# Two transformer blocks on one core: soft-MoE jobs interleaved with their neighbours, six PSUM banks in one ring

## The chip, the core and the metric

The kernel runs on one core of a Trainium2 chip. A core has five engines that run beside each other, each with an instruction queue of its own that it works off in order: TensorE (PE in the profile; its weight loads are listed as PEld), VectorE (DVE), ScalarE (ACT), GpSimd (POOL) and SyncE (SP, which here only issues DMAs). Matmul results go to PSUM, which holds eight banks of 128 partitions x 512 float32; every result has to be read out of its bank by DVE or ACT before the bank can take another.

The metric is the device time of one execution in microseconds; lower is better. The kernel before took 1081.13 us, the median of three runs (1080.82 to 1083.46).

## The reference

The input `x` is 8 sequences of 512 tokens, 128 channels. Two blocks follow each other; each normalises its input and adds the outputs of an attention and of a feed-forward part that both read the normalised rows. All is float32.

```python
xn = layernorm(x)
x = x + causal_attention_16_heads(xn) + soft_moe(xn)
xn = layernorm(x)
x = x + differential_attention(xn) + attention_and_top2_moe(xn)
```

The change touches the soft MoE of the first block. It has 8 experts of 64 slots each, so 512 slots:

```python
xn2 = rmsnorm(xn, norm_gamma);  sn = rmsnorm(slot_embeds, slot_norm_gamma)
logits   = einsum('bnd,esd->bnes', xn2, sn)      # per sequence: 512 tokens x 512 slots
dispatch = softmax(logits, over the tokens n)
combine  = softmax(logits, over all slots (e, s))
slots = einsum('bnd,bnes->besd', xn2, dispatch)
h  = gelu(einsum('besd,edh->besh', slots, w1) + b1)
eo = einsum('besh,ehd->besd', h, w2) + b2
out = einsum('bmd,bnm->bnd', eo, combine)
```

## The kernel before, in words

The program is written out in full by Python, in the order in which the code runs, and `in_order` (L244) ties every engine's instructions of the first part to that order. So the order in the text is the order on PE, DVE, ACT and POOL; what can differ is only how long each waits.

**Jobs.** For each of the 8 sequences (called batches, `b`) the soft MoE is two jobs. `dispatch(b)` (L326) returns five steps: `start` transposes the normalised rows (four 128x128 transposes into one bank, `xn2T_p`) and copies them to SBUF on ACT; `logits(k)` calls `soft` (L310) for blocks k and k+1: a matmul of 128 slots x 512 tokens into a bank (`lg`), the negated maximum of each row on DVE (`nm`), the exponential with its row sum on ACT (`ex`); `scale(k)` divides two blocks by their sums on DVE; `turn(k)` transposes two blocks (four transposes each into a bank, `dt`) and copies them on ACT into `disp`; `end` multiplies the rows by `disp` (`psl`, four matmuls that accumulate in a bank of the pool `o`) and writes the slots `slT` on DVE. `combine(b)` (L370) is alike with tokens as rows: `logits`, no scaling, `turn` (`ct`, copied to `comb` by ACT and DVE in turn) and `end`, which multiplies by the experts' outputs (`pf`) and adds to `x_all` on DVE.

Each `logits` or `turn` step handles two of the four blocks, so a job has two of each, with k = 0 and k = 2.

**The order of jobs.** `jobs` (L405) is a generator that runs a list of jobs as a pipeline of depth two: while `new` computes its logits, `last` is turned and ended. Each `yield` is a point at which others put in work of their own. `begin` (L415) starts the next dispatch, `rows_of` (L411) normalises the rows of the one after.

**Where jobs run.** Five stages, by their callers:
1. L542: dispatch 0 to 3, woven with `rest_in`, the layernorm statistics of batches 3 to 7. `weave` (L230) takes one step of each generator in turn.
2. L544: `slot_ffn(0)` (L454), the experts for the slots of batches 0 to 3, woven with dispatch 4 and 5 and with `late_in` (L517).
3. L545 to L590: the weights of the second block are folded, then combine 0, dispatch 6, combine 1, dispatch 7.
4. L592: `slot_ffn(1)` woven with combine 2 and 3.
5. L1163 to L1198: combine 4 to 7, with tiles from the pool `t`, beside the preparation of the first block's attention. The string at L1165 gives the order: each `p` is one piece of the preparation of batch 0 (`PREP`, L1019), each `c` one step of `jobs`; from L1194 four steps of `jobs` follow each group of four `m_head` calls (L1042, `sm`), until the jobs are done. There are nine such groups (`AHEAD`) before the first `e_head` (L1073, `se`), with which the attention proper begins. The preparation reduces squares and takes three Newton steps on DVE, transposes `q` and `k` (`qT_p`, `kT_p`), and ACT makes `qT` and `kj` of them.

**PSUM.** Three pools serve stages 1 to 4: `s` with four banks for logits and for the experts' hidden layer (`ph`), `o` with two banks for sums that build up over several matmuls (`psl`, `pf`, `pe`), `t` with two banks for transposes. A pool is a ring: a new tile takes the oldest bank and its first writer waits until that bank's last tile has been read. Stage 5 and the attention have other pools: seven banks `t` and one `o`.

The order of the steps in one round of `jobs` is this: both turns of `last`, then both logits of `new`, then the end of `last`:

```python
for k in (0, 2):
    if last: last[3](k); yield          # turn
for k in (0, 2):
    if new: new[1](k); ...; yield       # logits
if last: last[4](); yield               # end
```

Of the kernel before, what the change touches and what calls it, by code (L numbers as in the profile page):

```python
# [25 lines left out]
def kernel(ctx: ExitStack, tc: tile.TileContext, a: dict, out: bass.AP):  # L26
# [21 lines left out]
    ps = {}  # L48
# [189 lines left out]
                    runs.remove(r)  # L238

    fp = ExitStack()  # L240
    for k, n in (("s", 4), ("o", 2), ("t", 2)):
        ps[k] = fp.enter_context(tc.tile_pool(name=f"ps_{k}", bufs=n, space=PSUM))

    def in_order(start, end=None):  # L244

        free = mybir.DependencyInfo(mybir.DependencyClass.NoSync, mybir.DependencyReason.DATA)
        last = {}
        for ins in list(nc.cur_bb.bb.instructions)[start:end]:
            if ins.engine in engines:
                if ins.engine in last:  # L250
                    tc.add_manual_dep(ins, last[ins.engine], free, reason="order of the trace")
                last[ins.engine] = ins.name
# [69 lines left out]
    def xn2_in(b):  # L322
        ff["xn2", b] = xn2 = wkb.tile([P, NI, D], F32, tag="xn2", name=f"xn2_{b}", bufs=3)
        ln_apply0(b, 1, xn2)
# [80 lines left out]
    def jobs(todo):  # L405

        last = None
        ds = [b for kind, b in todo if kind is dispatch]
        made = {}

        def rows_of(b):  # L411
            if b is not None and ("xn2", b) not in ff:
                xn2_in(b)

        def begin(b):  # L415
            if b is not None and b not in made:
                rows_of(b)
                made[b] = dispatch(b)
                made[b][0]()

        def after_(b):
            n = ds.index(b) + 1 if b in ds else len(ds)
            return ds[n] if n < len(ds) else None

        if todo[0][0] is dispatch:
            begin(ds[0])
        for kind, b in todo + [(None, None)]:
            new = made[b] if kind is dispatch else kind(b) if kind else None
            nxt = None
            if kind is dispatch:  # L430
                nxt = after_(b)
            elif kind and ds and b is not None:
                nxt = next((d for d in ds if d not in made), None)
            for k in (0, 2):
                if last:
                    last[3](k)
                    yield
            for k in (0, 2):
                if new:
                    new[1](k)  # L440
                    if k == 0:
                        begin(nxt)
                    else:
                        rows_of(after_(nxt))
                        new[2](0)
                    yield
            if new:
                new[2](2)
            if last:
                last[4]()  # L450
                yield
            last = new
# [87 lines left out]
    ln_rows(2)  # L540
    ln_roots(2)
    weave((0, jobs([(dispatch, b) for b in range(HB)])), (1, rest_in()))  # L542
    l1_load()
    weave((0, slot_ffn(0)), (0, jobs([(dispatch, 4), (dispatch, 5)])), (0, late_in(range(6))))  # L544
    l1_fold()  # L545
    ac = {}
# [43 lines left out]
    for _ in jobs([(combine, 0), (dispatch, 6), (combine, 1), (dispatch, 7)]):  # L590
        pass
# [331 lines left out]
    with ExitStack() as at:  # L923
# [14 lines left out]
        for n in range(3):  # L938
            t = pads.tile([P, NI, PW * (2 * H + 1)], F32, name=f"vpad{n}")
# [3 lines left out]
        for n in range(4):  # L943
            t = pads.tile([P, NI, P], F32, name=f"mcol{n}")
# [636 lines left out]
```

## Time and profile before

| | |
|---|---|
| median of three runs | 1081.13 us (1080.82 to 1083.46) |
| profiled execution, its own time | 1080.87 us |
| its span, first to last instruction | 1079.2 us, mean granted clock 0.945 |
| stage 1, 10.4 to 64.1 us | 53.7 us, PE busy 43.27 |
| stage 2, 64.1 to 115.9 | 51.8 us, PE busy 49.66 |
| stage 3, 115.9 to 162.5 | 46.6 us, PE busy 39.74 |
| stage 4, 162.5 to 212.7 | 50.2 us, PE busy 48.20 |
| stage 5, 212.7 to 280.6, up to the first `se` | 67.9 us, PE busy 63.47 |
| a logit matmul (two passes of 592 ns that overlap), its maximum, its exponential | 0.86, 0.69, 0.69 us |
| four transposes into a bank, their copy on ACT | 0.52, 0.59 us |
| a table load on ACT (before a switch between exponential and Gelu) | 1.28 us |

How to read the profile: the page gives busy time by engine and in 40 slices of 27 us, with the granted clock of PE in tenths of full speed. A timeline lists an engine's instructions in order of time: start in us, duration in us, engine, line, operation, output and inputs with their shapes, how many were merged, and in brackets how long the engine stood idle before and which instruction ended that. Names leave out numbers (`dt` is any `dt_0_1`), and L141 is the line of the helper that records all transposes. A table of stretches gives the busy time of each engine in each stretch and the clock. Matmuls overlap in the pipeline, so durations of single ones do not add up; what adds up is the distance from start to start.

### The profile page before, as it was taken

Reading aid. Unit: us, or ns where it says so; the run is one execution under the profiler, and the core shown is the slowest. Engines: PE = TensorE matmul, PEld = TensorE weight load, DVE = VectorE, ACT = ScalarE, POOL = GpSimd, SP = SyncE. Lnnn points to the kernel's source line nnn. Section 1 sums busy time; section 2 is a strip of 40 time slices with the busy share of each in tenths; the row PEclk is TensorE's granted clock in tenths of the full one; section 3 lists DMA queues with packets and bytes.
Section 4 is the critical chain, followed back from the end, with each engine's and each line's share of the span. In section 5 each row is a group of like instructions: output and inputs, shape, how many; then the busy total and the mean of one; then the engine's idle time right before and its main releaser. Section 6 shows DMA issues by size and latency. Waiting matters only on the chain.

```text
span 1079.2 us, 18766 instructions
## 1 busy us (share of the span) xinstructions
PE 964.9 (89%) x6702; PEld 594.3 (55%) x6702; DVE 677.6 (63%) x2130; ACT 561.3 (52%) x1261; POOL 569.0 (53%) x794
## 2 busy tenths in 40 slices
PE   7889899989999999999899999878678879999990
PEld 3457556857545455545444445345445657777780
DVE  6634643377777788888878788359887642243230
ACT  3466347363366566767565655526346552393220
POOL 3201000200242537785878978876877635667775
PEclk9899999999699999999999999859889999999995
DMA  8630000000000000000000000050000143332213
GB/s 253 153 92 2 1 1 1 2 1 2 1 1 2 1 2 2 19 4 2 9 14 2 22 1 22 2 173 1 10 20 16 30 110 58 50 50 36 26 10 34
DMA packets 49838, 33.23 MB, mean 31 GB/s; under 512 B 12248, under 2 KB 44803, under 8 KB 49744
## 3 DMA queue, kind: packets, MB, share of 16 engines
q1 hardware_dynamic: 34832, 24.80, 8.6%
q0 software_dynamic: 14096, 6.97, 4.9%
q8 instruction: 53, 0.87, 0.3%
q14 instruction: 41, 0.34, 0.1%
q10 hardware_dynamic: 816, 0.26, 0.1%
HBM read 17.56 MB, written 17.33 MB: 32 GB/s over the span
## 4 chain that ended last, share of the span: by engine, by line
PE 62%; POOL 13%; DVE 13%; issue 5%; ACT 3%; DMA 2%; POOLq 0%; SPq 0%; DVEq 0%; ACTq 0%
PE se L1082 11%; PE phm L1458 6%; PE pem L1473 6%; PE po L1107 5%; PE sm L1049 4%; PE lg_d L316 3%; PE pe L491 3%; PE psl L360 3%; DVE junk L1059 3%; PE s L1287 3%; PE pf L393 2%; POOL xs L910 2%; PE pq L969 2%; PE lg_c L316 2%; PE ph L465 2%
## 5 line engine op out<-in xcount | busy, mean ns | idle before, releaser
L1059 DVE CUSTOM_DVE_ANT_0 junk<-sm,cmask 128x128 f32<-128x128 f32 (+3 forms) x512 | 249.7, 488 | 68.9 <-PE sm L1049 30.5
L1087 ACT ACTIVATE pt<-se 128x384 f32<-128x384 f32 (+1 forms) x384 | 185.7, 527 | 158.7 <-PE sm L1049 110.0
L1049 PE MATMUL sm<-kj,qT 32*128 32x256 f32 (+3 forms) x1024 | 231.5, 483 | 5.4 <-ACT kj L643 2.7
L1082 PE MATMUL se<-q,kj 32*128 32x128 f32 (+3 forms) x1024 | 210.2, 477 | 4.0 <-DVE mcol L1059 3.5
L1486 POOL DMA_INDIRECT out_dram<-es,to x80 | 124.4, 1555 | 61.9 <-issue 28.4
L1082 PEld LDWEIGHTS se<-q,kj 32*128 32x128 f32 x1024 | 99.8, 189 | 86.9 <-DVE mcol L1059 25.2
L1092 POOL TENSOR_SCALAR_AFFINE_SELECT pt<-pt 128x512 f32<-128x512 f32 (+1 forms) x96 | 80.0, 833 | 115.2 <-ACT pt L1087 115.0
L1049 PEld LDWEIGHTS sm<-kj,qT 32*128 32x128 f32 x1024 | 111.4, 190 | 24.4 <-DVE mcol L1059 10.3
L1107 PE MATMUL po<-pt,vpad 128*18 128x512 f32 (+3 forms) x1024 | 92.0, 455 | 12.0 <-POOL pt L1092 12.0
L1461 ACT ACTIVATE hTm<-phm 128x1024 f32<-128x1024 f32 (+1 forms) x48 | 42.4, 882 | 79.0 <-PE phm L1458 78.8
L1458 PE MATMUL phm<-xeT,w 128*128 128x512 f32 (+1 forms) x192 | 78.7, 534 | 4.1 <-DVE xeT L1447 3.6
L1473 PEld LDWEIGHTS pem<-w,hTm 128*128 128x128 f32 x640 | 77.0, 192 | 7.6 <-issue 7.2
L1291 ACT ACTIVATE ex<-s,nm 128x512 f32<-128x512 f32 x64 | 43.9, 687 | 69.2 <-DVE nm L1290 68.7
L1473 PE MATMUL pem<-w,hTm 128*128 128x128 f32 x640 | 78.9, 275 | 0.0
L910 POOL DMA_INDIRECT xs<-l_z,sput x64 | 67.3, 1051 | 17.9 <-issue 15.4
L1287 PE MATMUL s<-xn,qk 128*128 128x512 f32 x128 | 69.4, 662 | 7.1 <-ACT qk L1265 3.9
L522 POOL TENSOR_TENSOR x_all<-x_all,bo_bc 128x512 f32<-128x512 f32 x8 | 10.2, 1276 | 121.4 <-DVE xn L280 121.4
L1447 DVE TENSOR_SCALAR xeT<-xeT_p,cols 128x512 f32<-128x512 f32 (+1 forms) x24 | 17.2, 721 | 73.9 <-PE xeT_p L141 73.9
L1107 PEld LDWEIGHTS po<-pt,vpad 128*18 128x18 f32 x1024 | 20.7, 97 | 62.8 <-POOL pt L1092 23.7
L1290 DVE TENSOR_REDUCE nm<-s 128x1 f32<-128x512 f32 x64 | 43.0, 683 | 17.0 <-PE s L1287 16.7
L1458 PEld LDWEIGHTS phm<-xeT,w 128*128 128x128 f32 x192 | 34.0, 194 | 27.0 <-issue 21.6
L736 POOL TENSOR_TENSOR l_prod<-l_qkv 128x512 f32<-128x512 f32 x36 | 46.3, 1298 | 3.2 <-DVE l_at L630 1.9
(270 smaller groups left out, 1872.4 us busy)
## 6 DMA issues: line engine op xcount, KB each, us to landing
xs<-cmask SPq DMA_DIRECT2D x1, 5280.0 KB, 24.1
xe<-xs SPq DMA_DIRECT2D x8, 660.0 KB, 4.4
x_all<-in_L_attn_x_dram SPq DMA_DIRECT2D x8, 256.0 KB, 4.6
w<-in_L_ffn_w_dram SPq DMA_DIRECT2D x1, 2048.0 KB, 8.9
w<-in_L_ffn_moe_w_dram SPq DMA_DIRECT2D x1, 2048.0 KB, 9.8
out_dram<-x_all SPq DMA_DIRECT2D x8, 256.0 KB, 2.2
out_dram<-es,to POOLq DMA_INDIRECT x80, 3.2
xs<-l_z,sput POOLq DMA_INDIRECT x64, 2.3
```

Of the source, the lines that this page charges most:

```text
L316: nc.tensor.matmul(lg, lhsT=lhs(k), rhs=rhs, start=True, stop=True)
L910: put = nc.gpsimd.indirect_dma_start(out=xs, out_offset=bass.IndirectOffsetOnAxis(ap=sput[:, k, m : m + 1], axis=0), in_=z2[:, i], in_offs ...
L1049: nc.tensor.matmul(sc[:, o : o + w], lhsT=st["qT", b][rr, i * P : (i + 1) * P], rhs=st["k", b, j][rr, :w], start=True, stop=True,)
L1059: nc.vector.tensor_tensor_reduce(out=junk[:, :w], in0=sc[:, o : o + w], in1=cmask[:, 512 - w : 512], scale=-1.0, scalar=BIG, op0=ALU.add, ...
L1082: nc.tensor.matmul(sc[:, o : o + w], lhsT=st["k", b, j][rr, c * P : (c + 1) * P], rhs=st["q2", b, (g % G) // 2][rr, c * P : T], start=True ...
L1087: nc.scalar.activation(st["pt", g, k][:, r, :o], sc[:, :o], AF.Exp)
L1092: nc.gpsimd.affine_select(out=pt[:, :, :n, :P], in_=pt[:, :, :n, :P], pattern=[[0, 4], [0, n], [1, P]], compare_op=ALU.is_ge, fill=0.0, ba ...
L1107: nc.tensor.matmul(po[32 * r : 32 * r + 2 * PW, c * P : T], lhsT=vpads[b % 3][:, c, at_ : at_ + 2 * PW], rhs=pt[:, r, o : o + w], start=(c ...
L1287: nc.tensor.matmul(sc, lhsT=dd["qk", b, k][:, i * P : (i + 1) * P], rhs=xnT[:, b], start=True, stop=True)
L1458: nc.tensor.matmul(ph[:, k, :w], lhsT=w1_1[:, e, hc * P : (hc + 1) * P], rhs=xeT[:, :w], start=True, stop=True)
L1473: nc.tensor.matmul(pe[:, k * D : (k + 1) * D], lhsT=hT[:, hc, k * P : (k + 1) * P], rhs=w2_1[:, e, hc, :], start=(hc == 0), stop=(hc == NH ...
L1486: back = nc.gpsimd.indirect_dma_start(out=out_rows, out_offset=bass.IndirectOffsetOnAxis(ap=ee["to", e][:, c : c + 1], axis=0), in_=es[:, ...
```

## The change

It has two parts.

The pools `s` and `t` of stages 1 to 4 become one ring of six banks; `ps["s"]` is another name for it. So logits, the experts' hidden layer and transposes take banks in the order in which they are written in the program.

The round of `jobs` is reordered: first half of `new`'s logits, first turn of `last`, `begin` of the next dispatch, second turn of `last`, second half of `new`'s logits with the scaling and the rows of the one after, end of `last`. A round with both jobs now has six yields, where it had five, since `begin` has one of its own (also when there is nothing to begin). The weaving callers and the string at L1165 are as before, so their own steps fall between other steps of the jobs than before.

```diff
     fp = ExitStack()
-    for k, n in (("s", 4), ("o", 2), ("t", 2)):
+    for k, n in (("o", 2), ("t", 6)):
         ps[k] = fp.enter_context(tc.tile_pool(name=f"ps_{k}", bufs=n, space=PSUM))
+    ps["s"] = ps["t"]
...
-            for k in (0, 2):
-                if last:
-                    last[3](k)
-                    yield
-            for k in (0, 2):
-                if new:
-                    new[1](k)
-                    if k == 0:
-                        begin(nxt)
-                    else:
-                        rows_of(after_(nxt))
-                        new[2](0)
-                    yield
+            if new:
+                new[1](0)
+                yield
+            if last:
+                last[3](0)
+                yield
+            if new:
+                begin(nxt)
+                yield
+            if last:
+                last[3](2)
+                yield
+            if new:
+                new[1](2)
+                new[2](0)
+                rows_of(after_(nxt))
+                yield
             if new:
                 new[2](2)
             if last:
```

## The prediction

> **What bounds the kernel now.** I read the page first, for who is busy and at what clock; then the stretches table, cut at the borders of the stages that the change touches; then PE's timeline in those stages; then DVE's and ACT's, to see what PE waits for; last, the granted clock in steps of about 3.4 us around each halving.
>
> ```profile
> PE 964.9 (89%) x6702; PEld 594.3 (55%) x6702; DVE 677.6 (63%) x2130; ACT 561.3 (52%) x1261; POOL 569.0 (53%) x794
> PE   7889899989999999999899999878678879999990
> PEclk9899999999699999999999999859889999999995
> ```
>
> PE is busy for 89% of the span, and the first ten slices (27 us each) are no exception. Only its idle time and its slow clock can be won. The stages follow; columns are the stretch, its length, then busy us of PE, PEld, DVE, ACT and POOL, the granted clock, DMA.
>
> ```profile
> 10.40:64.10 53.70, 43.27 (x148) 23.52 (x148) 35.44 (x121) 24.70 (x54) 10.81 (x7) 0.90 0.81 203
> 64.10:115.90 51.80, 49.66 (x396) 36.34 (x396) 22.59 (x58) 32.69 (x65) 8.60 (x9) 1.00 0.01 2
> 115.90:162.50 46.60, 39.74 (x197) 25.39 (x196) 26.80 (x70) 23.26 (x53) 0.20 (x1) 1.00 0.00 1
> 162.50:212.70 50.20, 48.20 (x433) 39.21 (x433) 15.52 (x34) 28.18 (x58) 7.90 (x12) 1.00 0.00 1
> 212.70:280.60 67.90, 63.47 (x357) 43.70 (x357) 49.85 (x147) 27.72 (x72) 8.08 (x21) 0.90 0.00 1
> ```
>
> I call them S1 (dispatch jobs 0-3), S2 (slot experts, dispatch 4-5), S3 (fold, two combines, two dispatches), S4 (slot experts, combines 2-3) and S5 (combines 4-7 beside the preparation of the attention). PE stands idle 10.4, 2.1, 6.9, 2.0 and 4.4 us in them, and in S1 and S5 part of its work ran at half clock. From 280.6 on the order is the same in both kernels. PE's timeline shows where it waits (start, us, work, idle before it and who ended it):
>
> ```profile
> 33.67 1.07 PE L141 MATMUL dt<-ident,ex_d 128*128 128x128 f32 x8 [1.97 <-DVE ex_d L343]
> 36.24 1.94 PE L141 MATMUL dt<-ident,ex_d 128*128 128x128 f32 x8 [1.50 <-DVE ex_d L343]
> 37.97 3.62 PE L316 MATMUL lg_d<-xn2T,snT 128*128 128x512 f32 x4
> 43.83 3.60 PE L360 MATMUL psl<-disp,xn 128*128 128x512 f32 x8
> 53.01 3.60 PE L360 MATMUL psl<-disp,xn 128*128 128x512 f32 x8
> ...
> 72.38 1.00 PE L141 MATMUL xn2T_p<-ident,xn 128*128 128x128 f32 x4 [1.13 <-DVE xn L280]
> 128.07 1.10 PE L141 MATMUL ct<-ident,ex_c 128*128 128x128 f32 x8 [1.27 <-ACT comb L385]
> 172.87 1.98 PE L316 MATMUL lg_c<-snT,xn2T 128*128 128x512 f32 x4 [0.83 <-ACT hT L471]
> 232.47 1.51 PE L1049 MATMUL sm<-kj,qT 32*128 32x512 f32 x8 [2.70 <-ACT kj L643]
> ```
>
> In S1 the transposes wait for DVE's scaling (L343), which stands behind the layernorm statistics of later batches. The logits at 37.97 took 3.62 us where the pair takes 1.88 at full clock. The clock in the two places:
>
> ```profile
> 31.70:35.10 3.40, 1.07 (x9) 0.86 (x8) 3.15 (x14) 0.71 (x2) 0.00 (x0) 1.00 0.19 53
> 35.10:38.50 3.40, 2.26 (x9) 2.10 (x10) 3.19 (x15) 1.23 (x3) 1.00 (x1) 0.51 0.48 114
> 229.70:233.10 3.40, 0.70 (x9) 0.31 (x8) 1.53 (x5) 3.40 (x8) 0.00 (x0) 1.00 0.00 0
> 233.10:236.50 3.40, 3.40 (x20) 2.59 (x13) 2.10 (x6) 1.91 (x3) 0.00 (x0) 0.50 0.00 0
> ```
>
> A stretch of 3.4 us with about 1 us of PE work is followed by one at 0.50; each such stretch full of PE work costs 1.7 us.
>
> **The change, part by part.** Durations from the timelines: a logit 0.86 us of PE, its maximum 0.64 of DVE back to back, its exponential 0.69 of ACT (0.86 with the sum); four transposes 0.52, their copy 0.53; `psl` 3.44; `pf` 3.57. No instruction of these is added or removed; PE's, DVE's and ACT's are reordered. POOL's and SP's queues keep their order, and no DMA moves. ACT loads its table four times less (4 x 1.28 = 5.1 us), two in each slot stage; I cost that at nothing, as PE runs without a gap from 73.2 to 115 and ACT waits for it. Should PE wait there for `hT`, it would be worth up to 1.3 us each.
>
> The added waits: a neighbour's first two maxima now stand on DVE, and its first two exponentials on ACT, ahead of the copies of the job's own transposes. Behind those copies waits `psl` or `pf` on PE.
>
> *S1: -3.5.* I follow the new queues with the old durations. DVE: the first two maxima end at 15.9; statistics of batch 3 1.7; two maxima 1.3; scaling 1.05; the next rows 1.1; roots 0.3; scaling 1.05; job 1's two maxima 1.3: 23.5. ACT then ends their exponentials at 24.5 and makes five copies (four of `dt`, one of `xn2T`, 2.65): `psl` of job 0 starts at 27.2 (before 28.10). DVE goes on with two batches of statistics (4.0), two maxima 1.3, scaling 1.05, rows 1.1, statistics 1.7, scaling 1.0, slots 0.75 and roots 0.3, two maxima 1.3: 35.95. ACT adds exponentials and five copies: `psl` of job 1 at 39.7 (before 43.83). Job 2 is near PE's own pace: logits 1.72, four transposes 2.0, logits 1.72 and 0.25 of wait give 48.85 (before 53.01). The last one comes 2.85 us after the end of that (52.3): 55.15, before 59.59. So -4.4, if PE's clock is full throughout. As 1.07 us of transposes in a stretch was too little to keep the clock (31.7 to 35.1), I expect one or two halved stretches here too, mostly beside waits: 0 to 2 us back. Bounds -4.4 and -0.5 (a halved stretch under a whole `psl` as well); I take -3.5, nearer to the walk than to the clock's worst.
>
> *S2: -1.1.* Slots' up matmuls now stand where PE waited 1.13 us for the rows of batch 5. The 0.97 us ahead of the first logits (69.27) stays. The ring of six never stands: the bank six tiles back is read out several us earlier at each step.
>
> *S3: -1.25.* The 1.13 us at 123.20 stays, since the first combine has no neighbour. The 1.27 at 128.07 goes, and 0.24 to 0.29 at each second pair of transposes (four banks more). Late next is ACT: job 6's copies wait for the next job's exponentials, which costs 0.4 ahead of `psl`. Walked through, the four ends come 0.85, 0.7, 1.0 and 1.25 us earlier. Bounds -1.7 and -0.6.
>
> *S4: -1.2.* The waits of 0.35 (170.04) and 0.83 for a bank go: the ring is two deeper than the four that experts and logits shared.
>
> *S5: +3.0.* The combines now give three turns where they gave two, but the attention's pieces take seven turns as before. So `pf` of job 4 (3.57) and half of job 5's logits (1.72) move behind the first `sm`: 5.3 us. In front of it DVE's chain decides: last square at 219.3, sum and small steps 1.7, two maxima 1.3, Newton 3.6, two maxima 1.3, `q` 0.6, a copy 0.75, `k` 0.6: 229.1. Only two exponentials, two copies, `qT` 0.77 and `kj` 0.70 are left on ACT: `sm` starts at 230.65 (before 232.47). PE then has 5.3 - 1.8 = 3.5 us more to do up to the last `pf`. After that one group of `sm` fewer remains (2.84 of DVE) and no sum of squares (1.7), so the end of this sum is the old one within 0.7. But PE does only transposes between 220.9 and 230.65. That is two or three stretches like 229.7 to 233.1, so the clock stays halved until about 236.5: 5.9 us at half, of which 1.2 us is more than before's 3.4; and the combines' maxima and `sm`'s reductions meet each other on DVE, about 1 to 2.5 us by walking both queues. Bounds 0 and +5; I take +3.
>
> [...]
>
> From 280.6 on the work only shifts, but the halved stretch 270.6 to 287.7 covers 7.1 us of dense work there; it may end a stretch sooner or later: +-1.7, taken as 0.
>
> Sum: -3.5 - 1.1 - 1.25 - 1.2 + 3.0 = -4.05 on the profiled execution's 1080.87 (span 1079.2 and 1.67 around it): 1076.8. That execution lies 0.26 under the median 1081.13: **1077.1**.
>
> **Rivals.** 0.3%, about what a measurement of this kernel can tell from no change, is 3.2 us: 1077.9 and 1084.4 are the marks.
>
> *Flat.* S1 is bound by DVE's order and not by PE's, as its walk for job 0 shows (0.9 us won only); with S1 at its bound of -0.5 the sum is -1.05: 1080.1. For it: DVE was 3.15 of 3.4 us busy at 31.7. Against: the scaling comes up to 4 us earlier for job 1.
>
> *More.* S5 at its bound 0, S1 at -4.4: sum -7.95, 1073.2. For it: ACT had four exponentials ahead of `kj`. Against: the empty stretch on PE.
>
> *Slower: the clock.* Each job now waits in the ring for banks that its neighbour's exponentials hold (in S1's job 1 the last transposes wait 1.5 us), with only transposes around it. If that halves the clock in the dispatch and combine jobs, every stretch costs 1.7. It decides against the change from the third extra stretch on (4.05 / 1.7); five give 1077.1 + 8.5 = 1085.6. Against: in 130 to 160 us PE already stopped 0.24 to 0.29 us at each pair, at clock 1.00. [...]
>
> *Not what it says.* Five tiles of one job fill the ring, so interleaving hides nothing and each stage stays as it was; S5's shift alone would show: 1081 to 1084, part of the flat case.
>
> **Numbers.** Forecast 0.47, its own range 1074 to 1077.9; more 0.08; flat with the last 0.30; slower 0.15. So faster 0.55, same 0.30, slower 0.15. The range 1071.5 to 1084.4 leaves out the slower case and the far end of "more" (0.04).
>
> **What would show it.** S1's last `psl` at 54 to 57; no idle of 1.13 at `xn2T_p` in S2 and none of 0.83 at `lg_c` in S4; 26 table loads; in S5 idle of 4 us on PE ahead of `qT_p`, the first `sm` earlier and the clock at 0.50 after it; the first `se` 3 to 5 us earlier than 280.6. Wrong it is if S1 ends as before (DVE's order), if S5 gives away more than 5, or if halved stretches appear in S3.

## The result and the profile after

The changed kernel takes 1074.91 us (median of five runs, 1070.79 to 1079.17), the kernel before 1081.13: a ratio of 0.9934, 95% interval 0.9908 to 0.996. Measured once more in another group of runs it was 0.9922 (0.9908 to 0.9936). The runs of the kernel before lie at medians of 1081.1 to 1088.6 in the groups below, so kernels of different groups are compared by their ratios alone.

The profiled execution of the changed kernel is one of its longer runs, 1078.73 us (span 1077.0): the two profiles lie 2.14 us apart, the medians 6.22. The page's busy times, and PE's slices with the clock:

```profile
PE 967.1 (90%) x6702; PEld 595.5 (55%) x6702; DVE 676.2 (63%) x2130; ACT 553.5 (51%) x1257; POOL 567.6 (53%) x794
PE   7989899989999999999999999868678879999990
PEclk9999999989799999999998989879889999999995
```

ACT has four instructions less (26 table loads in place of 30) and PE as many as before. The clock was low in other slices than before (27 us each): the second slice, at 8 before, is at 9, the ninth (S5) fell to 8, and two slices of the attention loop further on, at 9 before, are at 8; the eleventh and the 27th rose from 6 and 5 to 7. The stages, cut at the same instructions as in the prediction:

```profile
10.27:59.49 49.22, 41.42 (x148) 21.65 (x148) 35.13 (x121) 23.55 (x54) 10.93 (x7) 0.97 0.79 194
59.49:109.19 49.70, 48.73 (x392) 36.05 (x393) 22.62 (x57) 30.15 (x63) 8.79 (x10) 1.00 0.13 28
109.19:155.76 46.57, 41.34 (x202) 26.24 (x200) 27.03 (x70) 22.34 (x53) 0.00 (x0) 0.96 0.00 1
155.76:204.26 48.50, 47.70 (x432) 39.49 (x432) 15.52 (x34) 27.23 (x57) 7.87 (x12) 1.00 0.01 1
204.26:275.21 70.95, 64.36 (x357) 42.37 (x357) 49.34 (x147) 26.22 (x71) 8.08 (x21) 0.88 0.00 1
```

S1 to S4 are shorter, S5 is longer. The first `se` comes at 275.21 instead of 280.60: 5.39 us won. Behind it, where both programs run the same instructions in the same order, this execution took 801.8 us and that of before 798.6. PE's timeline at the places that the prediction named:

```profile
36.12 1.12 PE L141 MATMUL dt<-ident,ex_d 128*128 128x128 f32 x4 [2.02 <-ACT ex_d L321]
39.77 3.60 PE L361 MATMUL psl<-disp,xn 128*128 128x512 f32 x8
54.95 3.70 PE L361 MATMUL psl<-disp,xn 128*128 128x512 f32 x8 [0.89 <-ACT disp L353]
69.89 0.83 PE L141 MATMUL xn2T_p<-ident,xn 128*128 128x128 f32 x4
219.29 1.11 PE L141 MATMUL qT_p<-ident,qk 128*128 128x128 f32 x4 [3.85 <-DVE qk L1003]
222.60 2.09 PE L1054 MATMUL sm<-kj,qT 32*128 32x512 f32 x8 [0.87 <-ACT kj L648]
227.95 3.74 PE L394 MATMUL pf<-eo,comb 128*128 128x128 f32 x32
```

The last `psl` of S1 starts at 54.95 (59.59 before). In S2 no idle time is left ahead of `xn2T_p` (1.13 before). In S5 PE now stands 3.85 us ahead of `qT_p`, and the first `pf` stands behind the first `sm`; before it stood ahead of it.

### The profile page after: what moved, and what is told of

Same layout as the page of the kernel before. It is cut to its first block, busy times and chain, and to the rows that moved or that the text cites. A ratio compares the mean times of both kernels' runs of the same rounds, so it can differ in the third digit from the quotient of the medians.

```text
span 1077.0 us, 18744 instructions
## 1 busy us (share of the span) xinstructions
PE 967.1 (90%) x6702; PEld 595.5 (55%) x6702; DVE 676.2 (63%) x2130; ACT 553.5 (51%) x1257; POOL 567.6 (53%) x794
## 4 chain that ended last, share of the span: by engine, by line
PE 63%; DVE 14%; POOL 12%; issue 5%; ACT 4%; DMA 2%; POOLq 0%; SPq 0%; DVEq 0%; ACTq 0%
PE se L1087 12%; PE pem L1478 6%; PE po L1112 5%; PE phm L1463 5%; PE sm L1054 4%; DVE junk L1064 3%; PE pe L496 3%; PE psl L361 3%; PE pf L394 3%; PE s L1292 3%; PE ph L470 3%; POOL xs L915 2%; PE lg_c L317 2%; PE pq L974 2%; POOL out_dram L1491 2%
## 5 line engine op out<-in xcount | busy, mean ns | idle before, releaser
L1054 PE MATMUL sm<-kj,qT 32*128 32x256 f32 (+3 forms) x1024 | 234.9, 488 | 2.1 <-DVE mcol L1064 1.3
L1087 PE MATMUL se<-q,kj 32*128 32x128 f32 (+3 forms) x1024 | 212.9, 481 | 4.2 <-DVE mcol L1064 3.8
L1112 PE MATMUL po<-pt,vpad 128*18 128x512 f32 (+3 forms) x1024 | 91.5, 453 | 10.9 <-POOL pt L1097 10.8
L527 POOL TENSOR_TENSOR x_all<-x_all,bo_bc 128x512 f32<-128x512 f32 x8 | 10.2, 1274 | 120.5 <-DVE xn L281 120.5
```

Of the source, the lines that this page charges most:

```text
L1054: nc.tensor.matmul(sc[:, o : o + w], lhsT=st["qT", b][rr, i * P : (i + 1) * P], rhs=st["k", b, j][rr, :w], start=True, stop=True,)
L1087: nc.tensor.matmul(sc[:, o : o + w], lhsT=st["k", b, j][rr, c * P : (c + 1) * P], rhs=st["q2", b, (g % G) // 2][rr, c * P : T], start=True ...
L1112: nc.tensor.matmul(po[32 * r : 32 * r + 2 * PW, c * P : T], lhsT=vpads[b % 3][:, c, at_ : at_ + 2 * PW], rhs=pt[:, r, o : o + w], start=(c ...
```

## Which part of the change moves which stage

Four kernels split the change. "Old round" and "new round" are the two orders of the steps in `jobs`; the new one is also called crossed. A halved stretch is one of about 3.4 us in which the granted clock is 0.50. The table at the end of the experiments has all stages of all kernels. In brackets stand the us at half clock by the clock's own records in the trace; behind the first `se` they are counted up to PE's last matmul, as the last 26 us hold no work of PE (1050.7 to 1077.0 in the changed kernel, 1052.8 to 1079.2 before).

**The ring alone.** The changed kernel with the old round:

```diff
-            if new:
-                new[1](0)
-                yield
-            if last:
-                last[3](0)
-                yield
...
+            for k in (0, 2):
+                if last:
+                    last[3](k)
+                    yield
+            for k in (0, 2):
+                if new:
+                    new[1](k)
...
```

> The ring of six with the old order of the round (transposes of both pairs, then logits). Stages are cut as in the prediction; the whole change took 4.65 us out of S1 (64.14 to 59.49 at the first slot expert), 1.42 out of S2, 0.70 out of S3, 1.66 out of S4, and put 3.04 into S5. Theory A, the order of the round is what moves S1 and S5, the ring only the waits for a bank: S1 within 0.6 of the old border (63.5 to 64.7), S5 within 0.7 of its old 67.9, S3 and S4 together 0.5 to 1.5 us shorter (the waits of 0.24 to 0.29 at the second pairs of transposes and of 0.35 and 0.83 at the combine's logits), S2 within 0.4: first exponential sum of the attention at 279 to 280.5 where it was 280.60, and a time 0 to 2 us under the kernel before. Theory B, the ring's extra banks carry the gain and the order is only what makes room for it: S1 at least 2.5 us shorter, and the first attention tile below 277.

**The order alone.** The changed kernel with the old pools:

```diff
-    for k, n in (("o", 2), ("t", 6)):
+    for k, n in (("s", 4), ("o", 2), ("t", 2)):
...
-    ps["s"] = ps["t"]
```

> The new order of the round with the old pools (four banks for logits and experts, two for transposes). Theory A, the order makes S1 and S5: S1 ends at 59.5 to 60.5, S5 takes 70 to 72 us as with the whole change, and S3 and S4 give back part of their gain (together 0.3 to 1.5 us longer than with the whole change): first attention tile at 275.5 to 277. Theory B, the extra banks carry it: S1 ends at 62 or later. Behind the first attention tile the program is the same in all kernels; it took 798.6 us in one profile and 801.8 in the other, which I put down to where the halved stretches of the clock fall, so the time itself may lie anywhere from 1071 to 1080.

The stages of the ring alone, then of the order alone (columns as above):

```profile
10.30:64.49 54.19, 44.10 (x149) 23.92 (x148) 35.49 (x120) 24.82 (x54) 10.64 (x7) 0.87 0.84 196
64.49:115.60 51.11, 49.10 (x392) 35.94 (x392) 22.01 (x57) 32.70 (x65) 8.08 (x7) 1.00 0.03 7
115.60:160.53 44.93, 39.59 (x203) 25.89 (x201) 27.22 (x70) 22.97 (x53) 0.73 (x4) 1.00 0.00 1
160.53:208.98 48.45, 47.66 (x432) 39.40 (x433) 15.33 (x34) 28.18 (x58) 7.89 (x12) 1.00 0.01 1
208.98:275.76 66.78, 62.20 (x357) 42.61 (x357) 49.60 (x147) 27.50 (x72) 8.09 (x21) 0.92 0.00 1
```

```profile
10.30:66.37 56.07, 42.78 (x148) 23.53 (x148) 35.36 (x121) 24.54 (x54) 10.86 (x7) 0.91 0.80 195
66.37:117.59 51.22, 49.26 (x392) 35.93 (x392) 22.62 (x57) 30.24 (x63) 8.79 (x10) 1.00 0.00 1
117.59:166.77 49.18, 40.66 (x202) 25.79 (x201) 27.02 (x70) 22.93 (x53) 0.00 (x0) 1.00 0.00 1
166.77:215.84 49.07, 48.04 (x433) 39.46 (x433) 15.53 (x34) 27.23 (x57) 7.87 (x12) 1.00 0.00 1
215.84:287.05 71.21, 64.63 (x357) 42.38 (x357) 49.32 (x147) 26.22 (x71) 8.07 (x21) 0.88 0.00 1
```

The ring alone measured 0.992 of the kernel before (0.9889 to 0.995), as much as the whole change; its first `se` is at 275.76, which theory A had at 279 or later and B below 277. A was right on S1 and S2 and B wrong on S1 (54.19, no gain), but the ring takes far more than A's 0.5 to 1.5 us out of S3 (47.27 to 44.93) and S4 (50.16 to 48.45), and S5 came 1.1 us below A's 67.9, with 10.7 us at half clock in place of 13.4. What the ring does in S3, one combine job shows, before and with the ring alone:

```profile
145.57 1.04 PE L141 MATMUL ct<-ident,ex_c 128*128 128x128 f32 x8
146.85 1.20 PE L141 MATMUL ct<-ident,ex_c 128*128 128x128 f32 x8 [0.24 <-ACT comb L385]
147.88 3.60 PE L316 MATMUL lg_d<-xn2T,snT 128*128 128x512 f32 x8
...
144.49 1.91 PE L141 MATMUL ct<-ident,ex_c 128*128 128x128 f32 x16
146.24 3.60 PE L317 MATMUL lg_d<-xn2T,snT 128*128 128x512 f32 x8
```

With two banks the second pair of transposes waits for the first pair's copies; with six it doesn't. From the first transpose to the next work it is 1.75 us instead of 2.31. The four jobs of S3 save 0.91, 0.50, 0.56 and 0.35 us in this way, 2.32 of the stage's 2.34.

The order alone measured 1.007 (1.0048 to 1.0092): slower, which neither theory had, though B's sign (S1 ending at 62 or later) came, with 66.37. It loses 2.2 us in S1 and 1.9 in S3. Why, PE's timeline of the order alone shows:

```profile
24.37 1.12 PE L141 MATMUL xn2T_p<-ident,xn 128*128 128x128 f32 x4 [4.08 <-ACT disp L352]
39.84 1.11 PE L141 MATMUL xn2T_p<-ident,xn 128*128 128x128 f32 x4 [4.75 <-ACT disp L352]
87.64 1.99 PE L469 MATMUL ph<-slT,w 128*128 128x256 f32 x8 [0.69 <-ACT ex_d L320]
109.09 1.14 PE L141 MATMUL dt<-ident,ex_d 128*128 128x128 f32 x8 [0.29 <-ACT disp L352]
```

The rows of the next job (`xn2T_p`) now stand between a job's two pairs of transposes, and need one of two banks. The banks hold the first pair, whose copies on ACT wait behind the neighbour's exponentials. So PE stops for 4.08 and 4.75 us. In S2 the 1.13 us ahead of `xn2T_p` is gone with the order alone too, but 0.69 and 0.29 us for banks come in its place (51.22 against 51.12). The order needs the banks, in S1 and in S2. S2 is also the one stage that only both parts together shorten (51.11 with the ring alone, 51.22 with the order alone, 49.70 with both).

**Old round in one stage.** `jobs(todo, crossed)` was given a flag; with `False` it plays the old round. In the first kernel only S5 has it:

```diff
-        rest = jobs([(last_combine, b) for b in range(4, NB)])
+        rest = jobs([(last_combine, b) for b in range(4, NB)], False)
```

> The whole change, except that the last four combines (S5) keep the old order of the round. Theory A, the 3.04 us lost in S5 come from the matmuls that the new order pushes behind the first sm, and from the clock halved in the empty stretch ahead of it: S5 is back to 67.9 within 0.7, with an idle time of PE under 3 us ahead of sm and one or two halved stretches around it in place of three, and the first attention tile comes at 272.2 (271.4 to 273). The time is then 2 to 4 us under the whole change's, about 1072, the spread of the clock behind it left aside. Theory B, S5 is longer because it starts at another point of the clock's own period (the halved stretches come on a grid of 3.41 us that does not start with the program) or because its inputs come in another order from S4: S5 stays at 70 to 71.

In the second only S1:

```diff
-    weave((0, jobs([(dispatch, b) for b in range(HB)])), (1, rest_in()))
+    weave((0, jobs([(dispatch, b) for b in range(HB)], False)), (1, rest_in()))
```

> The whole change, except that dispatch jobs 0 to 3 (S1) keep the old order of the round; the ring of six stays. Theory A, order alone makes S1's gain: the first slot expert starts at 63.5 to 64.5 (59.49 with the whole change), everything behind follows 4 to 5 us later, the first attention tile at 279 to 280.5. Theory B, the ring makes at least half of it: first slot expert at 62 or earlier. In both, a gain of 4.65 us there ought to show in the time as 2 to 6 us over the whole change's, since nothing behind S1 absorbs it.

With the old round in S5 it takes 66.76 us, the first `se` comes at 270.79, and the time is 0.9882 (0.985 to 0.9915). Theory A holds in its direction, with a price of 4.2 us rather than 3; S5 came 1.1 us below A's 67.9, and no halved stretch is left around the first `sm`. With the old round in S1 the first slot expert (`ph`) starts at 62.98, the first `se` at 276.88, and the time is 0.9951 (0.993 to 0.9972). That lies between theory A (63.5 or later) and theory B (62 or earlier), so this run decided nothing by itself. The reason is the clock: S1 is the same code here and in the ring alone, yet took 52.68 and 54.19 us, with 10.2 and 13.7 us at half clock. One more halved stretch is 1.5 us there.

## S5: an empty turn

The old round has five turns for two jobs, the new one six, since `begin` has one of its own even when there is no next dispatch. This kernel leaves that turn out in S5 and keeps the crossed order:

```diff
             if new:
                 begin(nxt)
-                yield
+                if not lean:
+                    yield
...
-        rest = jobs([(last_combine, b) for b in range(4, NB)])
+        rest = jobs([(last_combine, b) for b in range(4, NB)], True)
```

> The whole change, but in the last four combines the round has no turn of its own for the start of a next dispatch, of which there is none there. The crossed order of the round stays (first logits, transposes, second logits). Theory A: S5 lost 3 to 4 us because a round takes one turn more of the string, so that the first pf (3.6 us) and half of the next logits (1.7) fell behind the first sm; with the turn gone they are back ahead of it, S5 is 66.5 to 68 (70.95 with the whole change, 66.8 with the old round), the idle time ahead of qT_p is under 1 us, and the time is that of the kernel with the old round in S5 (0.988 of the kernel before) within 0.3%. Theory B: the crossing itself costs, as a neighbour's maxima and exponentials stand ahead of the copies that pf waits for: S5 stays at 69.5 to 71.

S5 took 67.50 us, the time was 0.9909 (0.9895 to 0.9923). PE's timeline of it:

```profile
216.02 1.13 PE L394 MATMUL pf<-eo,comb 128*128 128x128 f32 x8
218.88 2.94 PE L394 MATMUL pf<-eo,comb 128*128 128x128 f32 x24 [1.74 <-DVE comb L386]
221.66 0.60 PE L141 MATMUL qT_p<-ident,qk 128*128 128x128 f32 x4
224.09 1.14 PE L1055 MATMUL sm<-kj,qT 32*128 32x512 f32 x8 [1.40 <-ACT kj L649]
```

`pf` stands ahead of the first `sm` again and fills the time in which PE waited 3.85 us. So 3.4 of the 4.2 us came from the turn and 0.7 from the crossing (a wait of 1.74 within `pf`). The clock had no part in it: the old round's 66.76 and this 67.50 have 11.2 and 10.9 us at half clock, and with the new round S5 took 70.95, 70.90, 70.81 and 70.93 us in four profiles, with 17.7, 17.7, 11.0 and 17.7 us at half clock. With the old round the stage does go with the clock: 66.76 to 69.14 us, with 10.7 to 19.5 at half clock.

## The whole change again

The same kernel, run a second time.

> The whole change once more, unchanged, for a second profile and for times taken beside the three kernels that run with it. If the clock's halved stretches come on a grid that does not start with the program, as the profiles so far suggest, then the same code must give other numbers of them: S1 at 47.7 us plus 1.5 for each halved stretch in it (49.2 with one, 50.7 with two), S3 at 44.9 where no stretch is halved (46.57 with one in the first profile), S5 at 70 to 71, and 798 to 802 behind the first attention tile, more where more of it is halved. Rival: the numbers of the first profile belong to the program (S1 49.2, S3 46.6, S5 70.9, rest 801.8, each within 0.3), and the clock's stretches are at the same places again.

S1 took 50.07 us (its halved stretch lay on the first logits, from about 12.6, and not at 35.65), S3 46.59 (one halved stretch, as before), S5 70.90, the rest 800.65. So the place in S1 belongs to the execution. S3's came again, yet of the eight profiles that have the ring and the new round there, four show it and four have 44.9 us at full clock. Reading S1 as a fixed sum plus 1.5 per stretch missed by 0.9: what a halved stretch costs depends on what it covers.

## S1: where the statistics stand

In S1 `rest_in` weaves the layernorm statistics of batches 3 to 7 between the jobs' turns. DVE's timeline of the kernel before shows one batch between the two scalings of job 0 (its first and last lines):

```profile
18.64 0.88 DVE L343 TENSOR_SCALAR ex_d<-ex_d,rd 128x512 f32<-128x512 f32 x2
19.43 0.29 DVE L264 BATCH_NORM_STATS2 st_x<-x_all 128x6 f32<-128x128 f32 x1
...
20.94 0.18 DVE L265 BATCH_NORM_AGGREGATE mv_all<-st_x 128x2 f32<-128x6 f32 x1
21.04 0.13 DVE L340 RECIPROCAL rd<-sm_d 128x2 f32<-128x2 f32 x1
21.20 0.88 DVE L343 TENSOR_SCALAR ex_d<-ex_d,rd 128x512 f32<-128x512 f32 x2
```

The second pair of transposes waits for the second scaling: that is PE's 1.50 us. Job 1 has the same. The new round has its turns elsewhere, and there only job 1's scalings have a batch between them (the changed kernel; job 0's two scalings, then job 1's with the batch's first and last statistics between them):

```profile
18.50 0.88 DVE L344 TENSOR_SCALAR ex_d<-ex_d,rd 128x512 f32<-128x512 f32 x2
...
20.79 0.88 DVE L344 TENSOR_SCALAR ex_d<-ex_d,rd 128x512 f32<-128x512 f32 x2
...
28.18 0.88 DVE L344 TENSOR_SCALAR ex_d<-ex_d,rd 128x512 f32<-128x512 f32 x2
...
31.07 0.28 DVE L265 BATCH_NORM_STATS2 st_x<-x_all 128x6 f32<-128x128 f32 x1
...
32.58 0.18 DVE L266 BATCH_NORM_AGGREGATE mv_all<-st_x 128x2 f32<-128x6 f32 x1
32.67 0.13 DVE L341 RECIPROCAL rd<-sm_d 128x2 f32<-128x2 f32 x1
32.84 0.88 DVE L344 TENSOR_SCALAR ex_d<-ex_d,rd 128x512 f32<-128x512 f32 x2
```

Five kernels move the statistics against the turns: each `yield` of `rest_in` is doubled, and where it is said the first delay is 2 instead of 1.

```diff
             ln_rows(b)
             yield
+            yield
             ln_roots(b)
             yield
+            yield
```

First the ring with the old round, and the crossed round with the old one in S5, both with the delay of 1:

> The ring of six with the old order of the round (S1 54.19 and 52.68 in its two profiles, with four and three halved stretches: 48.2 plus 1.5 each), and the layernorm statistics of batches 3 to 7 spread over twice as many turns of S1, so that in jobs 0 and 1 half as many of them stand ahead of the scaling. It tells what the order of the round did in S1. Theory A, DVE's queue decides, as the prediction's walk had it: the matmuls psl of jobs 0 and 1 come 1 to 2 us earlier each, S1 is 1.5 to 3.5 us shorter (50 to 51.5 with two or three halved stretches), and it gives much of what the new order gave. Theory B, it is PE's order that decides (logits of the next job standing ready while the scaling runs): psl of jobs 0 and 1 within 0.7 of 27.9 and 43.6, S1 at 48.2 plus 1.5 a stretch again. In both the rest is as in the ring with the old order: S2 51.1, S3 44.9, S4 48.5, S5 66.8.

> The whole change, with the old round in the last combines (S5 66.8) and the statistics of S1 spread over twice as many turns. With the new order S1 is 47.7 plus 1.5 for each halved stretch. If DVE's queue still decides there, another 0.5 to 1.5 us go (psl of job 0 and 1 earlier than 26.2 and 39.8); if the logits and exponentials on ACT decide (the wait of 2.02 us for ex_d at 36.1 was put down to ACT), it stays within 0.5. The time is 0.985 to 0.99 of the kernel before, the lowest of all kernels here or level with that of the old round in S5.

S1 took 54.82 us in the first, no gain, and 47.78 in the second, a gain. It looked as if DVE mattered in the crossed round alone. But in the first the doubled turns had left a batch at the very same two places, and in the second they left none. So I placed them on purpose. Both kernels with the old round below have the delay of 2, which leaves none between the scalings of jobs 0 and 1; the third is the whole change with a batch in both places (delay 2, and one more `yield` behind `ln_roots`):

```diff
-    weave((0, jobs([(dispatch, b) for b in range(HB)])), (1, rest_in()))
+    weave((0, jobs([(dispatch, b) for b in range(HB)])), (2, rest_in()))
```

> The ring with the old order of the round, and the statistics of S1 spread and begun one turn later, so that no batch of them (1.6 us on DVE) stands between the two scalings of job 0 or of job 1; in the spread kernel before and in the kernel before the change one batch stood in each of the two places, in the changed kernel only in job 1's. Theory A, that place is what the order of the round changed in S1: PE's second waits of 1.50 for the scaling go in both jobs, psl of job 0 comes 1.5 and that of job 1 3 us earlier than with the ring alone, and S1 is 45.5 to 47.2 plus 1.5 for each halved stretch (48.2 plus 1.5 with the ring alone, 47.7 plus 1.5 with the whole change). Theory B, the crossed order itself carries it, since logits stand ready while the scaling runs: S1 stays at 48 or more plus 1.5 a stretch.

> The kernel before, with neither the ring nor the new order, and the same later statistics. Theory A: S1 falls by 2 to 3.5 us from 53.84 with as many halved stretches (three), the rest of the stages is as before (S2 51.1, S3 47.3, S4 50.2, S5 66.8 to 67.9), and the time is 0.997 to 0.9985 of the kernel before. Theory B, without six banks the second transposes wait for a bank anyway (0.29 us at each pair in jobs 2 and 3, so the price would be small): S1 falls by less than 1.

> The whole change with the statistics of S1 placed so that a batch of them stands between the two scalings of job 0 and of job 1 (in the whole change only in job 1). Theory A: psl of job 0 comes 1 to 1.6 us later than 26.2 (27.2 to 27.9 at full clock), and S1, spread as it is otherwise, is 49 to 50.5 plus what the clock takes, that is 1.5 to 3 over the 46.3 plus 1.5 a stretch of the crossed kernel with none there. Theory B: the crossed order covers it, S1 within 0.7 of 46.3 plus 1.5 a stretch.

PE's timeline of the ring with the old round and clear scalings:

```profile
19.12 2.06 PE L141 MATMUL dt<-ident,ex_d 128*128 128x128 f32 x16 [2.56 <-DVE ex_d L344]
24.89 3.60 PE L361 MATMUL psl<-disp,xn 128*128 128x512 f32 x8
30.46 3.05 PE L141 MATMUL dt<-ident,ex_d 128*128 128x128 f32 x16 [1.97 <-DVE ex_d L344]
37.78 3.60 PE L361 MATMUL psl<-disp,xn 128*128 128x512 f32 x8
```

Both waits of 1.50 are gone; those of 2.56 and 1.97 for the first scaling stay. And `psl` comes at 24.89 and 37.78, earlier than with the whole change (26.23, 39.77). S1 is 46.87 us, the time 0.9904 (0.9878 to 0.993). In the kernels with none between the scalings of jobs 0 and 1 a batch stands between job 2's (here at 39.65), but there PE does not wait: its 16 transposes from 41.21 have no gap. The kernel before with nothing but this gets S1 of 50.20 with two halved stretches in place of three, 3.6 us less, and 0.996 (0.9944 to 0.9975), though three halved stretches fell into its S3 in the profile (51.18). The whole change with a batch in both places takes 48.81 at full clock throughout, 2.5 us over what the crossed round with none has less its one halved stretch (47.78 - 1.5); its time is 0.9939 (0.992 to 0.9958). `psl` of job 0 came at 26.57, so there the crossing covered most of the batch; job 1 paid (wait of 1.75).

Less 1.5 us per halved stretch, S1 is: old round with two batches between scalings 48.2 and 48.2 (ring, S1 old) and 48.8; with none 45.4 (and 45.7 in the last kernel below); crossed with two 48.8, with one 47.7, 48.6, 47.7 and 47.6, with none 46.3. The place of the batches explains most of it, at 1.1 to 1.4 us a batch (1.7 from 48.8 to 45.4). Two of the sums (48.6 with one batch, 48.8 with two and the old round) stand 0.9 and 0.6 above their like, as what a halved stretch costs depends on what it covers. The crossed round as such is no better than the old: it keeps waits for ACT in place of those for DVE (1.08 and 1.15 us for `ex_d` at the last transposes of jobs 0 and 1 and 0.44 at their `psl`, in the crossed kernel with no batch between, S5 old, statistics spread). What is left of its gain is the clock: 3 or 4 halved stretches with two batches and the old round, 0 to 2 in all other kernels with the ring. But the old round with clear scalings is among those, with 1 and 2, so here too the crossing isn't needed.

## The parts together

The ring, in S1 the old round with clear scalings, in S2 to S4 the new round, in S5 the old one.

> The cheapest form of each stage found so far in one kernel: the ring of six; in S1 the old order of the round with no statistics between the scalings of jobs 0 and 1; in S2 to S4 the crossed order; in S5 the old order. If the stages add up, S1 is 45.4 plus 1.5 for each halved stretch (46.9 with one), S2 49.7, S3 44.9 (46.6 with a halved stretch), S4 48.5, S5 66.8 (69.1 with six halved stretches): the first attention tile at 267 to 271 where it was 280.6, and behind it 795 to 802 us. The time is then 0.984 to 0.989 of the kernel before and some 5 to 9 us under the whole change. If the stages don't add up, because a faster S1 only moves the halved stretches into S3 and S5, the first attention tile comes at 271 or later and the time is 0.989 or more.

The stages were as expected, at the upper end for their halved stretches: S1 48.70 with two halved stretches, S2 49.69, S3 44.91, S4 48.50, S5 69.12, so 9.4 us less up to the first `se`, at 271.22, just past the expected 267 to 271. Then it took 803.88 us, the longest of all profiles. The ratio is 0.9879 (0.9855 to 0.9903). That beats both kernels of the case, but it can't be told from the whole change with the old round in S5 (0.9882), nor from that with the statistics spread (0.9893) or the ring with clear scalings (0.9904).

All profiles (us; in brackets us at half clock; S1 from 10.3):

| kernel | S1 | S2 | S3 | S4 | S5 | first `se` | behind it | ratio |
|---|---|---|---|---|---|---|---|---|
| before | 53.84 (10.2) | 51.12 | 47.27 | 50.16 | 67.91 (13.4) | 280.60 | 798.6 (72.0) | 1 |
| whole change | 49.19 (3.4) | 49.70 | 46.57 (3.4) | 48.50 | 70.95 (17.7) | 275.21 | 801.8 (77.9) | 0.9934 |
| again | 50.07 (3.4) | 49.70 | 46.59 (3.4) | 48.49 | 70.90 (17.7) | 276.05 | 800.7 (81.3) | 0.9922 |
| ring alone | 54.19 (13.7) | 51.11 | 44.93 | 48.45 | 66.78 (10.7) | 275.76 | 797.6 (61.0) | 0.992 |
| order alone | 56.07 (10.2) | 51.22 | 49.18 | 49.07 | 71.21 (17.4) | 287.05 | 801.7 (85.0) | 1.007 |
| whole, S5 old | 50.63 (6.8) | 49.69 | 44.91 | 48.50 | 66.76 (11.2) | 270.79 | 801.4 (77.5) | 0.9882 |
| whole, S1 old | 52.68 (10.2) | 49.69 | 44.91 | 48.49 | 70.81 (11.0) | 276.88 | 798.2 (57.3) | 0.9951 |
| whole, no empty turn in S5 | 49.24 (3.4) | 49.69 | 46.59 (3.4) | 48.50 | 67.50 (10.9) | 271.82 | 795.7 (67.6) | 0.9909 |
| ring, statistics spread | 54.82 (13.7) | 51.12 | 44.94 | 48.45 | 67.94 (16.1) | 277.57 | 796.3 (55.6) | 0.9936 |
| S5 old, statistics spread | 47.78 (3.4) | 49.70 | 44.90 | 48.50 | 69.11 (19.5) | 270.29 | 798.9 (79.5) | 0.9893 |
| ring, clear scalings | 46.87 (3.4) | 51.12 | 46.58 (3.4) | 48.46 | 69.14 (19.5) | 272.47 | 797.1 (55.6) | 0.9904 |
| before, clear scalings | 50.20 (6.8) | 51.12 | 51.18 (10.2) | 50.17 | 66.78 (10.7) | 279.75 | 795.3 (61.0) | 0.996 |
| whole, batch in both scalings | 48.81 (0) | 49.70 | 46.60 (3.4) | 48.50 | 70.93 (17.7) | 274.84 | 797.5 (67.6) | 0.9939 |
| parts together | 48.70 (6.8) | 49.69 | 44.91 | 48.50 | 69.12 (19.5) | 271.22 | 803.9 (72.7) | 0.9879 |

## Why the prediction was right, and where it was not

The time, 1077.1, was 2.2 us too high, inside the forecast's own range, and the case (faster) was the one with the highest chance. The signs that it named came too: the last `psl` of S1 at 54.95, no idle time at `xn2T_p` in S2 and `lg_c` in S4, 26 table loads, 3.85 us ahead of `qT_p`, the first `se` 5.39 us earlier (it had 3 to 5). One of its signs of being wrong came as well, a halved stretch in S3. Step by step:

- **S1, -3.5.** Measured -4.65, and -3.77 the second time. The walk of DVE's queue gave `psl` at 27.2, 39.7, 48.85 and 55.15; they came at 26.23, 39.77, 48.61 and 54.95. The agreement from job 1 on is partly luck: the walk had the clock full, and the measured times have a halved stretch, from 35.65, ahead of them. For job 0 the walk's durations add up to 23.7 and not 23.5, and DVE was there at 22.87. That DVE's statistics ahead of the scaling bind the stage was right, and shown by moving them alone. What the walk didn't see is that this has little to do with the crossing: it is where `rest_in`'s turns fall between the round's. The step also allowed one or two halved stretches as an addition. There was one, but before there were three, so the clock was a part of the gain: about 3 of the 4.65 us by 1.5 a stretch.
- **S2, -1.1.** Measured -1.42, and the idle time at `xn2T_p` went as named. The ring is needed for it.
- **S3, -1.25.** Measured -0.70, within the bounds, but out of two errors. At full clock S3 is 2.36 us shorter, more than the bound. The term that was mis-sized is the wait for ACT's copies, taken as 0.4 ahead of each `psl`: in the kernel with the old round in S1 the wait at the second `psl` is 0.3 and at the others none but the last. Too small, on the other side, was what the banks save: an idle time of 0.24 ahead of a second pair of transposes costs 0.35 to 0.56 us from start to start. The reason given, four banks more, was right, and the ring alone makes the gain. Against it stands a halved stretch, named by the prediction only as a sign of being wrong. It follows on the fold (110.72 to 114.14, with waits of 1.24 and 1.01 that the kernel before has too), it came with the old round as well (ring, clear scalings), and half of the profiles with both parts don't have it; so it is no effect of the new order's waits.
- **S4, -1.2.** Measured -1.66; the ring alone gives -1.71. Right in its reason (waits for a bank), too low by half a us.
- **S5, +3.0.** Measured +3.04. The step that it started from, seven turns for more turns of the jobs, is the cause. The share given to the clock (1.2 us) isn't: 6.7 us less of half clock left the stage as long. The agreement in the sum is partly luck, as before itself lost 1.1 us to its clock in that profile (67.91 against 66.78).
- **Behind the first `se`, 0 within 1.7.** This step failed: 3.2 us were lost there in the profile. As the medians lie 6.22 us apart and the first `se` 5.39, the loss seems to belong to this execution, one of the longer ones, rather than to the kernel; what failed for certain is the bound. Over the 14 profiles the same instructions took 795.2 to 803.9 us. The time grows with the us at half clock, 0.19 us for each on a straight line through the 14 points (correlation 0.72, which shows no cause by itself). So the clock is likely a part of the spread, but at about a third of the price it would have were all of it under dense PE work (0.5 us for each us at a clock of 0.50, an estimate), and the longest of them (803.9) had only 72.7. The clock isn't all: one piece of 400 matmuls (420.89 to 466.54 before, 414.88 to 461.36 after) ran at full clock in all 14 profiles and took 45.6 or 45.7 us in eight and 46.5 to 47.7 in six; the changed kernel had 46.5 in one profile and 45.6 in the other. What moves it there stays open.

Of the rivals, *the clock* is not borne out: S2 and S4, where PE goes round the six banks most, ran at 1.00 in every profile with the ring. *Flat* had it right that DVE's order decides S1; that the new round changes this order, and takes the batch out of job 0's scalings, it left out. *More* had S1 right at its bound, but not S5. *Not what it says*, by which interleaving hides nothing, is refuted by S2 (49.70 against 51.11 with the ring alone).

## What to carry to other kernels

Of a change with two parts, one can carry the whole gain: split them before building on either, and cut both by stage, since here the total hid +3.0 in S5 under -8.4 in S1 to S4. When work is woven in by turns, count the turns: a turn that did nothing cost 3.4 us, and a filler between two halves of a step about 1.3, nearly the 1.4 that the reordering was worth in S2.

## What the runs showed of the hardware

In the traces the granted clock changed on a grid of 3.41 us (in the profiles of both kernels every stretch between two changes is a whole multiple of that, 3.41 to 211.6 us), and the grid does not start with the program: the same kernel had its halved stretch in S1 at 35.65 in one profile and at about 12.6 in the other. Cut on that grid, the changed kernel's stretches around its two first halvings are (columns as for the stages):

```profile
32.24:35.65 3.41, 1.35 (x11) 0.90 (x9) 3.31 (x11) 0.36 (x1) 0.91 (x1) 1.00 0.24 62
35.65:39.06 3.41, 2.94 (x7) 1.91 (x8) 2.07 (x12) 3.41 (x9) 1.84 (x2) 0.50 0.42 93
...
110.72:114.14 3.42, 2.04 (x13) 1.74 (x14) 1.73 (x9) 1.35 (x5) 0.00 (x0) 1.00 0.00 0
114.14:117.55 3.41, 3.41 (x4) 0.93 (x4) 1.64 (x10) 0.98 (x3) 0.00 (x0) 0.50 0.00 0
```

A stretch with 1.35 us of PE work, and one with 2.04, were followed by one at 0.50. In the 14 profiles, between 10 and 250 us, every stretch at full clock with up to 1.55 us of PE work was followed by a halved one, none with 2.1 us or more was, and between 1.64 and 2.06 both happened. Out of half clock it was the other way with a higher mark: up to 2.56 us of PE work it stayed at half, from 2.84 on it came back, with one exception at 3.28. So in these traces the halving goes with the PE work in the stretch, and not with the longest gap, which in these two was 2.02 and 1.24 us at most: the kernel before had a gap of 2.56 us from about 16.7, its stretch from 14.65 held 2.06 us of work, and the next one ran at full clock. From 260 us on the marks don't hold: in the changed kernel the profile has PE busy for 3.41 of 3.41 us from 264.41, where 32 `sm` take 7.21 us beside DVE's reductions (16 took 0.95 at 242.80), and the clock is at half from 267.82.
